# A two-layer graph network: both products with A2 by two levels of Strassen's scheme, streamed from DRAM, with outer sums of A2 made during the attention

## The chip, the core and the metric

The kernel runs on one core of a Trainium2 chip. A core has a matrix engine (TensorE; PE in the profile, its weight loads PEld), a vector engine (VectorE, DVE), an activation engine (ScalarE, ACT), a general engine (GpSimd, POOL) and a queue engine (SyncE, SP). SP and POOL issue the transfers between DRAM and the on-chip memory here, and 16 DMA engines carry them out. Each engine executes its own instructions in their order and waits on semaphores. The metric is the device time of one execution in microseconds; lower is better. All data are float32.

## What is computed

The reference, cut to what matters (N = 3327 rows, D = 512 columns):

```python
h = maximum(layernorm(x), 0)                         # layer 0: attention
q, k, v = h @ Wq.T + bq, h @ Wk.T + bk, h @ Wv.T + bv
x = x + softmax(q @ k.T / sqrt(512) + adj + adj) @ v
X = maximum(layernorm(x), 0)                         # layer 1: graph convolution
A2 = adj + eye(N)
dscale = diagonal(A2) ** -0.5
temp = A2 @ X @ W.T                                  # first product with A2
out = x + relu((dscale[:, None] * A2 * dscale[None, :]) @ temp)   # second
```

`adj` is N by N. The change concerns the two products with `A2`, each N by N times N by 512.

## The kernel before

The rows are cut into 26 tiles of 128 (the last has 127), the columns of `adj` into 7 chunks of 512 (the last has 255). The host also hands in `adjT`, the transpose of `adj`.

*Projection* (`merged`, `h_transposed`, `project`): layernorm, transposes and the products with the weights leave `hT`, `v` and `qh` on chip.

*Attention*, 26 tiles in a loop. `scores(i)` loads a row of `adj` chunks, multiplies (line 211), adds on VectorE (line 213) and takes the exponentials on ScalarE (line 220). The score chunks go through four PSUM buffers `mm`, so TensorE can be four chunks ahead of VectorE. `attend(i)` transposes the weights (line 235), copies each transposed chunk to `pT` on ScalarE or VectorE in turn (line 237), and multiplies with `v` (line 254). Then VectorE finishes the row (line 255), POOL stores it to `x1d` (line 75), and a layernorm follows whose power POOL computes (line 111); ScalarE writes the result into `qh`, where `h1(i)` finds it in layer 1. The loop calls `scores(i + 1)` before `attend(i)`.

*Layer 1*. The first product (line 312) runs over seven column chunks and 26 row tiles; `chunk` loads a 128 by 512 block of `adjT` and adds the identity where the block holds the diagonal (line 285). `temp` multiplies with `W` (line 299) and scales by `sd` = `dscale`. The second product (line 336) loads the same blocks again. At the end of each block ScalarE and VectorE finish four row tiles (lines 344, 345) and POOL stores them.

The kernel is written in the Tile framework: its scheduler fixes the order of each engine's instructions when the program is built, out of the order of the program, its own estimates of durations, and the number of buffers of each tile. A tile with `bufs=1` can't be written again before its last reader is done, a DMA among them.

Of the kernel before, what the change touches and what calls it, by code (L numbers as in the profile page):

```python
# [9 lines left out]
F32 = mybir.dt.float32  # L10
AF = mybir.ActivationFunctionType
ALU = mybir.AluOpType
AX = mybir.AxisListType

P = 128
BW = 512
EPS = 1e-5
LOWEST = -3.4028234e38


@with_exitstack
def graph_layers_kernel(
# [24 lines left out]
    nc = tc.nc  # L47
    N, D = x.shape
    DC = D // P
    NT = (N + P - 1) // P  # L50
    NB = (N + BW - 1) // BW
    TB = BW // P
    scale = 1.0 / math.sqrt(D)

    def rows(i):
        return min(P, N - i * P)

    def width(b):
        return min(BW, N - b * BW)

    def tiles_of(b):
        return range(b * TB, min(NT, (b + 1) * TB))
# [6 lines left out]
    def load(dst, src, n):  # L69
        for a, z in pieces(n):  # L70
            nc.sync.dma_start(dst[a:z], src[a:z])  # L71

    def store(dst, src, n):
        for a, z in pieces(n):
            nc.gpsimd.dma_start(dst[a:z], src[a:z])

    const = ctx.enter_context(tc.tile_pool(name="const", bufs=1))
    held = ctx.enter_context(tc.tile_pool(name="held", bufs=1))
    work = ctx.enter_context(tc.tile_pool(name="work", bufs=2))
    psum = ctx.enter_context(tc.tile_pool(name="psum", bufs=2, space=bass.MemoryType.PSUM))  # L80
    dram = ctx.enter_context(tc.tile_pool(name="dram", bufs=1, space=bass.MemoryType.DRAM))

    ident = const.tile([P, P], F32, name="ident")
    make_identity(nc, ident)
    mhalf = const.tile([P, 1], F32, name="mhalf")
# [7 lines left out]
    qh = [held.tile([P, DC, TB * P if b < NB - 1 else len(tiles_of(b)) * P], F32, name=f"qh{b}")  # L93
          for b in range(NB)]

    def h1(i):
        b, t = divmod(i, TB)
        return qh[b][: rows(i), :, t * P : (t + 1) * P]

    x1d = [dram.tile([rows(i), D], F32, name=f"x1d{i}") for i in range(NT)]  # L100

    def layernorm(dst, src, n):

        st = work.tile([P, 6], F32, name="st")
        nc.vector.bn_stats(st[:n], src)  # L105
        mv = work.tile([P, 2], F32, name="mv")
        nc.vector.bn_aggr(mv[:n], st[:n])
        ve = work.tile([P, 1], F32, name="ve")
        nc.vector.tensor_scalar(ve[:n], mv[:n, 1:2], EPS, None, op0=ALU.add)
        rstd = work.tile([P, 1], F32, name="rstd")  # L110
        nc.gpsimd.tensor_tensor(rstd[:n], ve[:n], mhalf[:n], op=ALU.pow)
        nc.vector.tensor_scalar(dst, src, mv[:n, 0:1], rstd[:n], op0=ALU.subtract, op1=ALU.mult)

    with tc.tile_pool(name="kv", bufs=1) as kv:
        hT = [kv.tile([P, DC, width(b)], F32, name=f"hT{b}") for b in range(NB)]
        v = [kv.tile([P, D], F32, name=f"v{i}") for i in range(NT)]


        with tc.tile_pool(name="proj", bufs=1) as proj:
# [5 lines left out]
            first = [load_x(i) for i in tiles_of(0)]  # L125
            w = {}
# [10 lines left out]
            u = proj.tile([P, DC], F32, name="u")  # L137
# [50 lines left out]
        att = ExitStack()  # L188
# [5 lines left out]
        def scores(i):  # L194
# [12 lines left out]
            for c in range(NB):  # L207
                wd = width(c)
                ps = psum.tile([P, BW], F32, name="mm", bufs=4)
                for d in range(DC):  # L210
                    nc.tensor.matmul(ps[:n, :wd], qh[qb][:, d, t * P : t * P + n], hT[c][:, d, :],  # L211
                                     start=d == 0, stop=d == DC - 1)
                nc.vector.tensor_tensor_reduce(ch[c][:n, :wd], ch[c][:n, :wd], ps[:n, :wd], 2.0, LOWEST,  # L213
                                               op0=ALU.add, op1=ALU.max, accum_out=mx[:n, c : c + 1])
# [28 lines left out]
        def attend(i):  # L243
            n = rows(i)
            _, xt, rs = S[i]
            ps = psum.tile([P, D], F32, name="av")
            sb = transposed(i, 0)
            for c in range(NB):
                now = sb
                if c + 1 < NB:  # L250
                    sb = transposed(i, c + 1)
                for k, j in enumerate(tiles_of(c)):
                    m = rows(j)
                    nc.tensor.matmul(ps[:n], now[:m, k, :n], v[j][:m], start=j == 0, stop=j == NT - 1)  # L254
            nc.vector.scalar_tensor_tensor(xt[:n], ps[:n], rs[:n], xt[:n], op0=ALU.mult, op1=ALU.add)
            store(x1d[i], xt[:n], n)
            y = work.tile([P, D], F32, name="y", bufs=1)
            layernorm(y[:n], xt[:n], n)
            nc.scalar.activation(h1(i), y[:n].rearrange("p (c e) -> p c e", c=DC), AF.Relu)
            del S[i]  # L260

        scores(0)
        for i in range(NT):
            if i + 1 < NT:
                scores(i + 1)
            attend(i)
        att.close()


    with tc.tile_pool(name="conv", bufs=1) as conv:  # L270
        w1 = conv.tile([P, DC, D], F32, name="w1")
        nc.sync.dma_start(w1, w1T.rearrange("(c p) o -> p c o", p=P))
        ts = [conv.tile([P, D], F32, name=f"ts{i}") for i in range(NT)]
        dg = [conv.tile([P, 1], F32, name=f"dg{i}") for i in range(NT)]
        sd = [conv.tile([P, 1], F32, name=f"sd{i}") for i in range(NT)]

        def chunk(j, b, diagonal):

            m, wd = rows(j), width(b)
            a = conv.tile([P, BW], F32, name="a", bufs=12)  # L280
            load(a[:m, :wd], adjT[j * P : j * P + m, b * BW : b * BW + wd], m)
            if j // TB == b:
                t = j % TB
                blk = a[:m, t * P : t * P + m]
                nc.vector.tensor_add(blk, blk, ident[:m, :m])  # L285
                if diagonal:
                    junk = conv.tile([P, P], F32, name="junk", bufs=2)
                    nc.vector.scalar_tensor_tensor(junk[:m, :m], blk, 1.0, ident[:m, :m], op0=ALU.mult,
                                                   op1=ALU.mult, accum_out=dg[j][:m])
                    nc.gpsimd.tensor_tensor(sd[j][:m], dg[j][:m], mhalf[:m], op=ALU.pow)  # L290
            return a

        def temp(b, axt):

            for i in tiles_of(b):
                n, t = rows(i), i % TB
                ps = psum.tile([P, D], F32, name="av")
                for d in range(DC):
                    nc.tensor.matmul(ps[:n], axt[:, d, t * P : t * P + n], w1[:, d, :],  # L299
                                     start=d == 0, stop=d == DC - 1)  # L300
                nc.vector.tensor_scalar(ts[i][:n], ps[:n], sd[i][:n], None, op0=ALU.mult)


        waiting = None
        for b in range(NB):
            wd = width(b)
            acc = [psum.tile([P, BW], F32, name="mm", bufs=4) for _ in range(DC)]
            for j in range(NT):
                m = rows(j)
                a = chunk(j, b, True)  # L310
                for d in range(DC):
                    nc.tensor.matmul(acc[d][:, :wd], h1(j)[:, d, :], a[:m, :wd],  # L312
                                     start=j == 0, stop=j == NT - 1)
                if j == 1 and waiting:
                    temp(*waiting)
            axt = conv.tile([P, DC, BW], F32, name="axt", bufs=2)
            for d in range(DC):
                cp = nc.vector.tensor_copy if d % 2 else nc.scalar.copy
                cp(axt[:, d, :wd], acc[d][:, :wd])  # L319
            waiting = b, axt  # L320


        for b in range(NB):
            its = tiles_of(b)
            acc = [psum.tile([P, D], F32, name="mm", bufs=4) for _ in its]
            res = []
            for i in its:
                xr = conv.tile([P, D], F32, name="x1", bufs=8)
                load(xr, x1d[i], rows(i))
                res.append(xr)  # L330
            for j in range(NT):
                m = rows(j)
                a = chunk(j, b, False)
                for t, i in enumerate(its):
                    n = rows(i)
                    nc.tensor.matmul(acc[t][:n], a[:m, t * P : t * P + n], ts[j][:m],  # L336
                                     start=j == 0, stop=j == NT - 1)
                if j == 1 and waiting:
                    temp(*waiting)
                    waiting = None  # L340
            for t, i in enumerate(its):
                n = rows(i)
                r = conv.tile([P, D], F32, name="r", bufs=4)
                nc.scalar.activation(r[:n], acc[t][:n], AF.Relu, scale=sd[i][:n])  # L344
                nc.vector.tensor_add(r[:n], r[:n], res[t][:n])
                store(out[i * P : i * P + n], r[:n], n)


# [35 lines left out]
```

## Time and profile before

| | |
|---|---|
| Time, median of 3 runs (lowest, highest) | 2730.26 us (2728.12, 2731.69) |
| The profiled execution | 2727.29 us; span of its core 2724.9 us; mean granted TensorE clock 0.997 |
| Projection | up to 213 us of the span |
| Attention, 26 tiles, one each 47.50 us | to 1456 us |
| Idle TensorE at the start of layer 1 | 7.53 us (to 1463.8 us) |
| First product (line 312), busy | 584.4 us |
| Product with `W` (line 299), busy | 90.4 us |
| Second product (line 336), busy | 580.6 us |
| DMA over the span | 172.5 MB, mean 63 GB/s |

"Busy" is the time in which at least one instruction of a group ran; "mean ns of one" is longer for matmuls, since they overlap. A float32 matmul is two MATMUL instructions in the profile (a transpose is one): the 1352 of line 336 are 676 products of a 128 by 128 weight with 512 columns. "Idle before" is the idle time of the engine ahead of a group, with what ended it. The last columns of a row of the windows are the granted TensorE clock (1.00 is full speed), the busy share of the DMA engines and their GB/s.

### The profile page before, as it was taken

To read this page: it belongs to the slowest core of one execution; us is meant where nothing else is said; L and a number is where in the kernel's file an instruction comes from. 1 tells how busy PE (TensorE), PEld (TensorE's weight loads), DVE (VectorE), ACT (ScalarE), POOL (GpSimd) and SP (SyncE) were. 2 spreads that over 40 slices of the span, in tenths; PEclk is the share of its full clock that TensorE was granted. 3 is DMA by queue.
4 is the path that set the end of the run, shared out by engine and by line. 5 is a ranking of instruction groups with operands and counts; after the bars stand their busy time and mean duration, and the time that the engine had idled before them with its cause. 6 is when DMAs were issued, how large, how long until landed. Compare 5 with 4: busy or idle time off the path is not lost.

```text
span 2724.9 us, 17898 instructions
## 1 busy us (share of the span) xinstructions
PE 2697.8 (99%) x7100; PEld 1277.0 (47%) x7100; DVE 387.0 (14%) x983; ACT 237.1 (9%) x591; POOL 74.6 (3%) x138
## 2 busy tenths in 40 slices
PE   8999999999999999999998999999999999999998
PEld 4445444444444445444444444444446544444443
DVE  3322121212122121221211000000000000000000
ACT  1001111121111112111110000000000000000000
POOL 1000000000000000000000000000000000000000
PEclk9999999999999999999999999999999999999999
DMA  3001111111111111111103222222221332333322
GB/s 120 31 8 62 47 41 56 43 52 47 44 51 44 51 41 53 47 47 52 41 25 131 78 62 62 77 60 61 77 56 45 93 106 81 103 108 108 99 65 60
DMA packets 96900, 172.54 MB, mean 63 GB/s; under 512 B 11434, under 2 KB 21415, under 8 KB 96816
## 3 DMA queue, kind: packets, MB, share of 16 engines
q1 hardware_dynamic: 92592, 157.77, 20.4%
q0 software_dynamic: 4224, 13.63, 1.3%
q8 instruction: 55, 0.90, 0.1%
q14 instruction: 29, 0.24, 0.0%
HBM read 157.73 MB, written 13.63 MB: 63 GB/s over the span
## 4 chain that ended last, share of the span: by engine, by line
PE 99%; DMA 1%; DVE 0%; SPq 0%; ACT 0%; issue 0%; POOL 0%; POOLq 0%; ACTq 0%
PE mm L312 21%; PE av L254 21%; PE mm L211 21%; PE mm L336 21%; PE av L299 3%; PE av L176 3%; PE mm L168 3%; PE tp L235 3%; PE mm L143 1%; DMA wk<-in_wk_dram 0%; PE tp L160 0%; DMA a<-in_adjT_dram 0%; PE mm L149 0%; SPq L71 0%; DVE st L105 0%
## 5 line engine op out<-in xcount | busy, mean ns | idle before, releaser
L254 PE MATMUL av<-v,pT 128*128 128x512 f32 (+2 forms) x1352 | 606.2, 593 | 0.6 <-ACT pT L237 0.6
L312 PE MATMUL mm<-a,qh 128*128 128x512 f32 (+3 forms) x1456 | 584.4, 564 | 7.5 <-DVE a L285 7.5
L211 PE MATMUL mm<-hT,qh 128*128 128x512 f32 (+3 forms) x1456 | 588.5, 561 | 0.0
L336 PE MATMUL mm<-ts,a 128*128 128x512 f32 (+2 forms) x1352 | 580.6, 592 | 0.0
L312 PEld LDWEIGHTS mm<-a,qh 128*128 128x128 f32 (+1 forms) x1456 | 277.6, 191 | 314.2 <-issue 308.9
L211 PEld LDWEIGHTS mm<-hT,qh 128*128 128x128 f32 (+1 forms) x1456 | 274.5, 190 | 303.4 <-issue 299.0
L336 PEld LDWEIGHTS mm<-ts,a 128*128 128x128 f32 (+2 forms) x1352 | 256.8, 190 | 323.0 <-issue 323.0
L254 PEld LDWEIGHTS av<-v,pT 128*128 128x128 f32 (+2 forms) x1352 | 246.5, 190 | 261.4 <-issue 254.1
L213 DVE CUSTOM_DVE_ANT_0 s<-s,mm 128x512 f32<-128x512 f32 (+2 forms) x182 | 117.8, 647 | 373.8 <-PE mm L211 370.8
L220 ACT ACTIVATE s<-s,nmx 128x512 f32<-128x512 f32 (+2 forms) x182 | 123.1, 681 | 63.7 <-DVE nmx L216 63.7
L237 ACT COPY pT<-tp 128x512 f32<-128x512 f32 (+1 forms) x104 | 52.1, 501 | 823.7 <-PE tp L235 823.7
L235 PEld LDWEIGHTS tp<-ident,s 128*128 128x128 f32 (+2 forms) x676 | 84.8, 142 | 71.7 <-issue 68.9
L235 PE MATMUL tp<-ident,s 128*128 128x128 f32 (+2 forms) x676 | 99.3, 273 | 0.0
L237 DVE COPY pT<-tp 128x512 f32<-128x512 f32 (+1 forms) x78 | 53.9, 692 | 278.9 <-PE tp L235 278.9
L168 PE MATMUL mm<-hT,M 128*128 128x512 f32 (+1 forms) x224 | 91.5, 562 | 0.0
L299 PE MATMUL av<-w,axt 128*128 128x512 f32 (+1 forms) x208 | 90.4, 592 | 0.0
L176 PE MATMUL av<-wv,hT 128*128 128x512 f32 (+1 forms) x208 | 90.4, 592 | 0.0
L285 DVE TENSOR_TENSOR a<-a,ident 128x128 f32<-128x128 f32 (+1 forms) x52 | 15.2, 292 | 523.7 <-DMA a<-in_adjT_dram 506.7
L344 ACT ACTIVATE r<-mm,sd 128x512 f32<-128x512 f32 (+1 forms) x26 | 17.9, 687 | 570.0 <-PE mm L336 570.0
L319 ACT COPY axt<-mm 128x512 f32<-128x512 f32 (+1 forms) x14 | 7.8, 556 | 661.5 <-PE mm L312 661.5
L299 PEld LDWEIGHTS av<-w,axt 128*128 128x128 f32 (+1 forms) x208 | 39.5, 190 | 49.3 <-issue 49.3
L176 PEld LDWEIGHTS av<-wv,hT 128*128 128x128 f32 (+1 forms) x208 | 39.5, 190 | 49.3 <-issue 49.3
(43 smaller groups left out, 471.2 us busy)
## 6 DMA issues: line engine op xcount, KB each, us to landing
a<-in_adjT_dram SPq DMA_DIRECT2D x300, 256.0 KB, 2.6
s<-in_adj_dram SPq DMA_DIRECT2D x150, 256.0 KB, 2.6
xt<-in_x_dram SPq DMA_DIRECT2D x25, 256.0 KB, 3.0
xr<-in_x_dram SPq DMA_DIRECT2D x25, 256.0 KB, 2.5
x1d<-xr POOLq DMA_DIRECT2D x25, 256.0 KB, 2.3
x<-x1d SPq DMA_DIRECT2D x25, 256.0 KB, 4.2
out_dram<-r POOLq DMA_DIRECT2D x25, 256.0 KB, 4.3
a<-in_adjT_dram SPq DMA_DIRECT2D x50, 127.5 KB, 2.0
```

Source lines behind the costliest of these rows:

```text
L143: nc.tensor.matmul(ps, w["q"][:, c, r * P : (r + 1) * P], w["k"][:, c, :], start=c == 0, stop=c == DC - 1)
L168: nc.tensor.matmul(ps[:, :wd], M[:, c, o * P : (o + 1) * P], hT[b][:, c, :wd], start=c == 0, stop=c == DC - 1)
L176: nc.tensor.matmul(ps[:n], hT[b][:, c, t * P : t * P + n], w["v"][:, c, :], start=c == 0, stop=c == DC - 1)
L211: nc.tensor.matmul(ps[:n, :wd], qh[qb][:, d, t * P : t * P + n], hT[c][:, d, :], start=d == 0, stop=d == DC - 1)
L213: nc.vector.tensor_tensor_reduce(ch[c][:n, :wd], ch[c][:n, :wd], ps[:n, :wd], 2.0, LOWEST, op0=ALU.add, op1=ALU.max, accum_out=mx[:n, c : ...
L220: nc.scalar.activation(ch[c][:n, :wd], ch[c][:n, :wd], AF.Exp, bias=nmx[:n], accum_out=sums[:n, c : c + 1])
L235: nc.tensor.transpose(pt[:m, k, :n], S[i][0][c][:n, k * P : k * P + m], ident[:n, :n])
L237: cp(sb[:, :full, :n], pt[:, :full, :n])
L254: nc.tensor.matmul(ps[:n], now[:m, k, :n], v[j][:m], start=j == 0, stop=j == NT - 1)
L299: nc.tensor.matmul(ps[:n], axt[:, d, t * P : t * P + n], w1[:, d, :], start=d == 0, stop=d == DC - 1)
L312: nc.tensor.matmul(acc[d][:, :wd], h1(j)[:, d, :], a[:m, :wd], start=j == 0, stop=j == NT - 1)
L336: nc.tensor.matmul(acc[t][:n], a[:m, t * P : t * P + n], ts[j][:m], start=j == 0, stop=j == NT - 1)
```

## The change

`adjT` comes in padded with zeros to 3328 by 3328. `A2` is cut twice into 2 by 2, and each level multiplies with seven block products instead of eight, by Winograd's form of Strassen's scheme.

- *Outer sums of A2* (`sums_unit`): four sums of blocks, `S1` to `S4`, made once during the attention, in 104 units of 208 columns: two loads, three additions, one store to `sumd`. Four units follow each `attend` in the program.
- *Outer and inner sums of the right-hand side* (`right_hand`): for each of seven outer products and each pair of row tiles, eight 128-column blocks, stored to `rhs`. Those of the first product follow `attend` of tiles 19 to 24 and the end of the attention; those of the second are made between the steps of layer 1, out of the results of `temp`.
- *Layer 1* (`Step`, `gather`): two products, two halves of the rows, seven outer products, and for each seven steps: six of two row tiles and one of one. A step loads its block of `A2` (or its sum) and of `rhs`, makes the inner sums of `A2` on VectorE, and multiplies 416 columns at a time into seven PSUM banks, one for each inner product (`p8` besides for the last step). `gather` adds the seven banks up into `ct`. `temp` and `finish` use the bank `p8` too; `finish` transposes `ct` back for the output.

The diff, cut to its core:

```diff
+ORDER = ("p5", "p1", "p6", "p7", "p2", "p3", "p4")
+HALF = 13; PAIRS = 6; HW = HALF * P; XW = HW // 2; QW = HW // 4; CW = 208
+    def sums_unit(pool, s, j, c):
+        g = pool.tile([P, 4, CW], F32, name="g")
+        for y in range(2):
...
+            nc.sync.dma_start(g[:, 2 * y : 2 * y + 2, :], src[:, :, c : c + CW])
+            for x in range(2):
+                with_diagonal(g[:, 2 * y + x, :], r0, c0 + x * XW)
+        o = pool.tile([P, 4, CW], F32, name="o")
+        nc.vector.tensor_add(o[:, 0:2, :], g[:, 0:4:3, :], g[:, 1:2, :].to_broadcast([P, 2, CW]))
+        nc.vector.tensor_add(o[:, 2, :], o[:, 1, :], g[:, 0, :])
+        nc.vector.tensor_add(o[:, 3, :], o[:, 2, :], g[:, 2, :])
+        nc.gpsimd.dma_start(sumd[s][j][:, :, c : c + CW], o)
+    def inner(bt):
+        nc.vector.tensor_sub(bt[:, 4], bt[:, 0], bt[:, 1])
...
+    def right_hand(pool, g, products, t, row, written=()):
+        for r in products:
+            what = B_OF[r]
+            if what not in ("T2", "T4"):
+                bt = pool.tile([P, 8, P], F32, name="bt")
+            for k, i in enumerate((HALF - 1,) if t is None else (t, t + PAIRS)):
+                outer(bt[:, 2 * k : 2 * k + 2], what, lambda: row(i), lambda: row(HALF + i))
...
+                inner(bt)
+                nc.gpsimd.dma_start(rhs[g][r][t], bt)
 
+        presum = att.enter_context(tc.tile_pool(name="presum", bufs=1))
             attend(i)
+            for unit in units[i * per_tile : (i + 1) * per_tile]:
+                sums_unit(presum, *unit)
+            if HALF + PAIRS <= i < HALF + 2 * PAIRS:
+                right_hand(presum, 0, ("p5", "p6", "p4", "p1", "p7", "p2", "p3"), i - HALF - PAIRS, h1)
+        right_hand(presum, 0, ("p5", "p6", "p4", "p1", "p7", "p2", "p3"), None, h1)
...
+        with nc.allow_non_contiguous_dma(reason="the diagonal, once"):
+            nc.sync.dma_start(dg, bass.AP(..., ap=[[LD + 1, P], [P * (LD + 1), NT]]))
+            def sums(self):
+                o = self.o = conv.tile([P, 4, QW], F32, name="o", bufs=3)
+                nc.vector.tensor_add(o[:, 0:2, :], a[:, 0:4:3, :], a[:, 1:2, :].to_broadcast([P, 2, QW]))
+                nc.vector.tensor_add(o[:, 2, :], o[:, 1, :], a[:, 0, :])
+                nc.vector.tensor_add(o[:, 3, :], o[:, 2, :], a[:, 2, :])
+            def multiply(self, ps):
...
+                for r, i, m in (
+                    ("p1", 0, a[:, 0, 0]), ("p6", 5, o[:, 2]), ("p7", 6, o[:, 0]), ("p5", 4, o[:, 1]),
+                    ("p2", 2, a[:, 1, 0]), ("p3", 3, o[:, 3]), ("p4", 7, a[:, 1, 1]),
+                ):
+                    nc.tensor.matmul(ps[r][:, :QW], b[:, i], m, ...)
+        def gather(ct, r, ps):
...
+        def finish(ct, i):
+            xr = conv.tile([P, D], F32, name="x1", bufs=2)
+            load(xr, x1d[i], n)
+            pt = banks.tile([P, DC, P], F32, name="p8")
+            for d in range(DC):
+                nc.tensor.transpose(pt[:, d, :], ct[:, d, k * P : (k + 1) * P], ident)
+            o = conv.tile([P, D], F32, name="r", bufs=2)
+            nc.scalar.activation(o[:n], ..., AF.Relu, scale=sd[:n, i : i + 1])
+            nc.vector.tensor_add(o[:n], o[:n], xr[:n])
+            store(out[i * P : i * P + n], o[:n], n)
+        def more(t):
+            temp(cts[0, 1], i)
+            if t is not None:
+                temp(cts[0, 1], i + PAIRS)
+            right_hand(conv, 1, ("p5", *late), t, ts.get, written=("p5",))
+        for k in range(HALF):
+            at(per + k * PAIRS // HALF, lambda k: temp(cts[0, 0], k), k)
+            at(3 * per + k * PAIRS // HALF, lambda k: finish(cts[1, 0], k), k)
+        for k, t in enumerate((*range(PAIRS), None)):
+            at(per + PAIRS + 1 + k, lambda t: right_hand(conv, 1, early, t, ts.get), t)
+            at(2 * per + min(k, PAIRS - 1), more, t)
```

`outer` makes 256 columns with one instruction, of VectorE or (for `B11`, `B21`, `B22`) ScalarE, and `inner` four times 128 columns on VectorE. A step of one row tile multiplies four times 416 columns. `gather` is one copy on ScalarE, eight sums of 416 columns on VectorE and then none, one or three of 1664 columns. In `conv`, `bt` has one buffer, `a` and `b` have six, and `ts` of the second half of the rows has three. The four nested loops of steps call `load` two steps ahead and `sums` one step ahead.

## The prediction

> **What bounds the kernel now.** First the page: busy times, the chain that ended last, the costliest groups.
>
> ```profile
> PE 2697.8 (99%) x7100; PEld 1277.0 (47%) x7100; DVE 387.0 (14%) x983; ACT 237.1 (9%) x591; POOL 74.6 (3%) x138
> ...
> q1 hardware_dynamic: 92592, 157.77, 20.4%
> ...
> PE 99%; DMA 1%; DVE 0%; SPq 0%; ACT 0%; issue 0%; POOL 0%; POOLq 0%; ACTq 0%
> ...
> L312 PE MATMUL mm<-a,qh 128*128 128x512 f32 (+3 forms) x1456 | 584.4, 564 | 7.5 <-DVE a L285 7.5
> ...
> L336 PE MATMUL mm<-ts,a 128*128 128x512 f32 (+2 forms) x1352 | 580.6, 592 | 0.0
> L235 PE MATMUL tp<-ident,s 128*128 128x128 f32 (+2 forms) x676 | 99.3, 273 | 0.0
> ```
>
> TensorE is 99% of the path; the two products of the change take 1165.0 us, with one idle gap of 7.5 us. Nothing else is late: VectorE has 14%. A saved product is saved time, as long as TensorE stays the last.
>
> Second, the groups with their shapes apart, for unit prices; third, the windows; fourth, the DMA view and two lines of the timeline, for what the change leans on and this kernel hardly uses, round trips through DRAM.
>
> ```profile
> L312 PE MATMUL mm<-a,qh 128*128 128x255 f32 x200 | 43.3, 378 | 0.0
> L285 DVE TENSOR_TENSOR a<-a,ident 128x128 f32<-128x128 f32 x50 | 14.6, 292 | 520.7 <-DMA a<-in_adjT_dram 503.7 <-issue 16.7
> L345 DVE TENSOR_TENSOR r<-r,x 128x512 f32<-128x512 f32 x25 | 17.3, 693 | 284.5 <-ACT r L344 284.5
> ```
> ```profile
> 1456.00:1464.00 8.00, 0.47 (x2) 0.23 (x2) 2.88 (x8) 0.63 (x1) 1.68 (x3) 0.70 0.77 259
> 1464.00:1470.00 6.00, 6.00 (x8) 2.47 (x9) 1.81 (x11) 0.00 (x0) 2.55 (x4) 0.54 1.03 390
> ```
> ```profile
> x1d<-xr POOLq DMA_DIRECT2D x25, 256.0 KB, 2.3
> ...
> out_dram<-r POOLq DMA_DIRECT2D x25, 256.0 KB, 4.3
> ...
> x1d<-xr POOLq DMA_DIRECT2D x1, 224.0 KB, 7.0
> ```
> ```profile
> 1003.39 0.75 DVE L255 SCALAR_TENSOR_TENSOR xr<-av,rs,xr 128x512 f32<-128x512 f32 x1 [8.05 <-PE av L254]
> 1004.44 0.58 POOL L75 DMA_DIRECT2D x1d<-xr  x1 [45.95 <-DVE xr L255]
> ```
>
> The windows give 390 GB/s for saturated loads, and a clock of 0.54 behind the 7.5 us gap. A store alone lands in 2.3 us; the same store issued while the loads of layer 1 stream took 7.0. From the end of VectorE's instruction to POOL's issue pass 0.30 us.
>
> **Matmuls.** The built program has 1288 matmuls of 416 columns: 28 outer products of 6 x 7 + 4. A product of 512 columns takes 580.6/676 = 0.859 us, one of 255 takes 43.3/100 = 0.433; a line through them gives 0.700 for 416, so 902 us. `temp` is unchanged (208 MATMULs). The output's 104 transposes at 99.3/676 = 0.147 add 15. TensorE: 902 + 15 - 1165 = **-248**.
>
> VectorE's additions, by L285 and L345, cost 0.158 us + 1.044 ns per column: 0.59 for 416, 0.375 for 208, 0.425 for 256, 1.03 for 832, 1.9 for 1664. Per outer product, 6 x 2.2 of inner sums, 4.8 of `gather` and at most 5.7 of 1664-column sums are 24 us beside 32 us of matmuls: hidden. I allow 0.4 us at each of 28 changes of banks: **+10** (0 to 40).
>
> **Sums of A2 in the attention.** `g` and `o` have one buffer, so unit follows unit: additions 0.59 + 2 x 0.375 and gaps, 1.4 us; then the next addition waits on VectorE's own queue for the later of two round trips. Store: 0.30 + 2.3 for 256 KB + 0.4 for 416 KB at 390 GB/s = 3.0. Loads: two issues and 2.6 = 3.2. A unit is 4.7 us if the two don't disturb each other; each has 416 KB, 1.1 us, and in line it is 5.8; with the 7.0 row it would be 8.7. I take 5.9, near the middle row, because both start together and the loads of `adj` come between. Behind the waiting addition stand the `pT` copies of line 237, the score reductions of line 213 and line 255, so TensorE waits for them after its four buffers. The order of the built program has 13 units before the end of the first tile, ten in each of the next nine, one after. Ten take 59 us, a tile has 47.5 (in the chain in order of time line 211 starts anew at 290.86, 338.36, 385.86): 9 x 11.5, and some 6 in the first tile: **+110** (0 at 4.7 us, +210 at 7).
>
> **Sums of the right-hand side, tiles 19 to 25.** Seven a tile through one `bt`: 0.85 outer and 1.33 inner, then 0.30 + 2.3 + 0.7 for 512 KB; 5.5 us each, 38.5 of 47.5. Hidden but for late copies: **+10** (0; 60 at the middle row).
>
> **Start of layer 1.** All loads of layer 1 wait for the last `right_hand`, since they take the memory of the first layer's pools. From the last product with `v`: row end and layernorm 3.3 us (timeline), one piece with its store 4.6, seven short pieces in series at about 2.6: the last ends at 25. Then `w1` (1 MB), 3328 single elements of the diagonal (no row shows such a load; 0 to 10 us, I take 3, it is small), and 1.4 MB for the first step, 6 us at 390 GB/s, and 6 of latency and first sums: 40 against 7.5 now: **+33** (25 to 45).
>
> **Right-hand sums in layer 1.** They again have one `bt`, and VectorE's queue holds the inner sums of the next steps behind them. (a) Twelve long pieces in outer products 7 and 8; stores beside a stream take 4.3 to 7.0 us, so a piece is 7 to 9 us where a step of 4.9 (11.8 with `temp`) is planned: **+20** (5 to 50). (b) In outer products 14 and 15 the built order puts 26 long pieces ahead of the sums for the third step of product 15, and its `p8` matmul behind the last `temp`. Nine lie beside TensorE's work there. Seventeen remain at 5.5, with 0.9 more for each rebuilt `T1`: 97 us, beside 24 us of `temp`; with the clock and the nine being slower than planned: **+81** (50 to 110). (c) The remaining nine pieces **+12** (0 to 30), and `finish` beside steps **+7** (0 to 15).
>
> **End.** Now 8 us pass from the last matmul to the end. Then `gather` ends at 3, and 13 `finish` go through two `r` buffers: ScalarE 0.69, VectorE 0.69, store 2.6, handovers 0.3, halved: 2.1 us each, 27; then a store and the end, 6: **+29** (20 to 40).
>
> The stream itself: a step loads 0.85 MB of `A2` and 0.52 of `rhs` per 4.9 us, 281 GB/s, 72% of the 390 seen. I price it at nothing; the six buffers cover it.
>
> **The Trainium skill beside this.** "DMA: Bandwidth & Descriptors", "Issuing engines are not separate DMA queues": transfers started by different engines share the 16 engines and interleave; it agrees with the 2.3 and 7.0 rows and speaks against the change. The same page, "Anatomy of one DMA", gives about 2.0 us + bytes/436 GB/s for a store; by that, an estimate, the unit's store is 3.0 us whatever else runs, a unit 4.7, and the attention's term 0. "TensorE: Matmul & The Clock Gate", Part 1, halves the clock after an idle window of about 3.4 us; here 7.5 us idle gave 0.54 in the window behind it. By the rule an idle of 7 us in a tile costs some 3 us more; where VectorE sets the pace, that is hidden.
>
> **Sum.** -248 + 10 + 110 + 10 + 33 + 20 + 81 + 12 + 7 + 29 = +64. The profiled execution took 2727.3 us (2724.9 of span and 2.4 around it), 3.0 less than the median of the three runs: 2727.3 + 64 + 3 = **2794**.
>
> **Rivals.** *Faster: the round trips hide.* With 4.7 us a unit the attention loses nothing, and with 3.3 us for every store the terms of layer 1 are 5, 55, 5 and 0; start 25, end 22, banks 0: -248 + 112 = -136, 2594. For it: the 2.3 row is the median of 25 stores, and the scheduler's order of ten units a tile is what it thinks fits. Against it: the 4.3 and 7.0 rows. The rest unchanged, it decides at a unit of 5.2 us: there the sum is zero. *Slower still: the stream is the bound.* The queue of loads has 20.4% of 16 engines' span for 157.77 MB, 284 GB/s while busy; were that all that a mix of loads and stores reaches, the 901 us would stretch by a tenth or more: +100, 2894. Against it: 390 in the window. *It doesn't do what it says*: 1288 matmuls stand in the built program, so no.
>
> **How the numbers follow.** Forecast 0.60; round trips hide, 0.25 (between 2594 and no change); stream bound 0.12; no change 0.03. So faster by over 0.2% (5.5 us, about what a measurement of this kernel can tell from no change) 0.25, within 0.03, slower 0.72. Range: the attention's term alone spans 210 us, that of (b) 60. Low 2660, which holds the upper half of the hiding case; high 2900, with the stream-bound case.
>
> **What would show it.** Right: matmuls of 902 us; in the first ten tiles a period of 55 to 64 us with TensorE waiting for VectorE (`pT`), whose additions wait for the store of `o`; a hole of 60 to 100 us in the middle of layer 1; 40 us idle at its start; no hole in the steady outer products. Wrong: a period of 47.5 in all tiles, or steps longer than 4.9 us that wait for `a` or `b`.

## The result and the profile after

The changed kernel takes 2838.07 us (median of 4 runs, 2836.17 to 2842.04) beside 2729.70 before (4 runs, 2728.12 to 2731.69): a ratio of 1.0399, 95% interval 1.0381 to 1.0417. It is slower by 108 us, where 64 were predicted (2794 us). The spans of the two profiled executions differ by 2838.1 - 2724.9 = 113.2 us, and the working below is made against these.

First the page of the changed kernel: busy times, the loads' queue, the chain, and the costliest groups.

```profile
PE 2542.8 (90%) x6972; PEld 1271.4 (45%) x6972; DVE 1149.7 (41%) x2471; ACT 271.9 (10%) x683; POOL 190.7 (7%) x315
...
q1 hardware_dynamic: 180540, 360.37, 39.3%
...
issue 15%; POOL 1%; DMA 0%; POOLq 0%; DVE 0%; ACT 0%; ACTq 0%
...
L345 PE MATMUL av<-v,pT 128*128 128x512 f32 (+2 forms) x1352 | 651.2, 629 | 90.3 <-DVE pT L328 89.0
L302 PE MATMUL mm<-hT,qh 128*128 128x512 f32 (+3 forms) x1456 | 596.3, 566 | 37.2 <-DVE mx L304 37.1
L441 PE MATMUL p<-o,b 128*128 128x416 f32 x1344 | 533.4, 517 | 8.1 <-DVE ct L458 5.1
L441 PE MATMUL p<-a,b 128*128 128x416 f32 x1008 | 417.5, 516 | 48.4 <-DVE o L427 39.7
...
L145 DVE TENSOR_TENSOR o<-g 128x416 f32<-128x416 f32 x104 | 61.6, 592 | 316.2 <-DMA sum<-o 270.1
```

TensorE, 99% busy before, now has 90%. The new products (line 441) are cheaper than the old ones, but TensorE now waits for VectorE in the attention (lines 345 and 302), where before it was idle for 0.3 us in all. VectorE in turn stood idle for 270.1 us ahead of the first additions of the units (line 145), until the store of `o` had landed. The chain is of no use here: it runs from the end back along POOL's queue of stores and loses its way ("issue 15%"). What TensorE waited for says it better:

```profile
PE av L345 <- DVE pT L328: 89.0, 22, 8.6
PE p L481 <- DVE ts L483: 63.3, 11, 18.1
PE p L441 <- DVE o L427: 39.7, 1, 39.7
PE mm L302 <- DVE mx L304: 37.1, 18, 4.8
PE p L492 <- ACT r L494: 24.1, 18, 2.9
```

These are the places of the prediction: the units in the attention (first and fourth row), the hole of outer products 14 to 17 (`ts`), the start of layer 1 (one wait of 39.7), the `finish` steps. Outer products are numbered from 0, as in the prediction. The windows put the waits in time; the columns after the engines' busy times are the granted clock, the DMA engines' busy share and GB/s.

```profile
452.10:518.90 66.80, 53.76 (x133) 24.87 (x132) 22.24 (x60) 7.53 (x20) 8.24 (x13) 0.90 0.51 161
955.90:1003.40 47.50, 47.50 (x136) 23.07 (x135) 9.39 (x26) 7.43 (x20) 1.11 (x2) 1.00 0.17 48
...
1647.80:1686.30 38.50, 0.04 (x1) 0.07 (x1) 6.78 (x18) 2.45 (x6) 11.02 (x13) 0.53 0.45 142
...
1753.00:1913.60 160.60, 160.60 (x461) 87.40 (x460) 97.72 (x137) 2.53 (x5) 0.00 (x0) 1.00 0.81 282
...
2255.10:2383.20 128.10, 67.88 (x149) 31.01 (x148) 48.30 (x148) 6.89 (x19) 11.16 (x21) 0.77 0.39 152
...
2796.70:2838.10 41.40, 13.44 (x53) 8.53 (x52) 11.39 (x15) 8.93 (x13) 7.54 (x14) 0.55 0.47 152
```

A tile with units (first row) takes 66.8 us and TensorE works in 53.8 of them; a tile without (second) takes the old 47.5 and TensorE fills it. Five outer products without other work (fourth) take 160.6, TensorE never idle. The third row is the start, the fifth outer product 15, the last the end. Last, one unit in the timeline, and where its transfers land:

```profile
478.40 0.59 DVE L145 TENSOR_TENSOR o<-g 128x416 f32<-128x416 f32 x1 [4.29 <-DMA sum<-o]
...
479.44 0.38 DVE L147 TENSOR_TENSOR o<-o,g 128x208 f32<-128x208 f32 x1
...
479.84 0.88 SPq L140 DMA_DIRECT2D g<-in_adjT_dram  x2
...
480.11 0.71 POOL L148 DMA_DIRECT2D sum<-o  x1 [5.60 <-DVE o L147]
...
484.71 0.59 DVE L145 TENSOR_TENSOR o<-g 128x416 f32<-128x416 f32 x1 [1.40 <-DMA sum<-o]
```
```profile
g<-in_adjT_dram SPq DMA_DIRECT2D x208, 208.0 KB, 3.1
sum<-o POOLq DMA_DIRECT2D x104, 416.0 KB, 4.6
```

From addition to addition 6.31 us pass here. Over the units after the thirteenth the mean is 6.63 (the median 6.38): 1.55 from the first addition's start to the last one's end (a reduction of the scores, line 304, slips in between at times), 0.33 to POOL's issue, 4.60 to the landing, 0.15 to the next addition. Ten of these are the 66.3 us of a tile.

### The profile page after: what moved, and what is told of

It reads as the page before. It is cut to its first block, busy times and chain, and to the rows that moved or that the text cites. A ratio compares the mean times of both kernels' runs of the same rounds, so it can differ in the third digit from the quotient of the medians.

```text
span 2838.1 us, 20558 instructions
## 1 busy us (share of the span) xinstructions
PE 2542.8 (90%) x6972; PEld 1271.4 (45%) x6972; DVE 1149.7 (41%) x2471; ACT 271.9 (10%) x683; POOL 190.7 (7%) x315
## 5 line engine op out<-in xcount | busy, mean ns | idle before, releaser
L345 PE MATMUL av<-v,pT 128*128 128x512 f32 (+2 forms) x1352 | 651.2, 629 | 90.3 <-DVE pT L328 89.0
L441 PE MATMUL p<-o,b 128*128 128x416 f32 x1344 | 533.4, 517 | 8.1 <-DVE ct L458 5.1
L441 PE MATMUL p<-a,b 128*128 128x416 f32 x1008 | 417.5, 516 | 48.4 <-DVE o L427 39.7
L441 PEld LDWEIGHTS p<-o,b 128*128 128x128 f32 x1344 | 256.7, 192 | 227.5 <-issue 201.2
L441 PEld LDWEIGHTS p<-a,b 128*128 128x128 f32 x1008 | 191.8, 191 | 210.9 <-issue 154.1
L425 DVE TENSOR_TENSOR o<-a 128x832 f32<-128x832 f32 x168 | 172.1, 1024 | 251.6 <-PE p L441 181.0
L145 DVE TENSOR_TENSOR o<-g 128x416 f32<-128x416 f32 x104 | 61.6, 592 | 316.2 <-DMA sum<-o 270.1
L481 PE MATMUL p<-w,ct 128*128 128x512 f32 x208 | 104.2, 648 | 63.3 <-DVE ts L483 63.3
L148 POOL DMA_DIRECT2D sum<-o x104 | 74.4, 715 | 667.5 <-DVE o L147 546.6
L426 DVE TENSOR_TENSOR o<-o,a 128x416 f32<-128x416 f32 x168 | 99.3, 591 | 4.8
L427 DVE TENSOR_TENSOR o<-o,a 128x416 f32<-128x416 f32 x168 | 99.2, 591 | 4.7
L328 DVE COPY pT<-tp 128x512 f32<-128x512 f32 (+1 forms) x78 | 53.6, 687 | 112.6 <-PE tp L326 112.6
```

Of the source, the lines that this page charges most:

```text
L328: cp(sb[:, :full, :n], pt[:, :full, :n])
L425: nc.vector.tensor_add(o[:, 0:2, :], a[:, 0:4:3, :], a[:, 1:2, :].to_broadcast([P, 2, QW]))
L426: nc.vector.tensor_add(o[:, 2, :], o[:, 1, :], a[:, 0, :])
L427: nc.vector.tensor_add(o[:, 3, :], o[:, 2, :], a[:, 2, :])
L441: nc.tensor.matmul(ps[r][:, :QW], b[:, i], m, start=self.t == 0, stop=self.t == PAIRS - 1 and r in ("p1", "p5", "p6", "p7"))
L481: nc.tensor.matmul(ps, ct[:, d, k * P : (k + 1) * P], w1[:, d, :], start=d == 0, stop=d == DC - 1)
```

## The experiments

The stage readings below are made alike for each run: the attention ends where VectorE's last row end does, layer 1 runs from its first matmul to its last outer product's, and the end is what follows. The change itself: attention to 1647.8, start 38.4, layer 1 1110.5, end 41.4. The attention's end differs by up to 10 us between runs that have the same code there (1640.3 to 1649.9). Where no number of runs is given, a time is that of one run; the kernel before took 2727.8 to 2730.9 beside them.

### Six units a tile

```diff
-        per_tile = -(-len(units) // NT)
+        per_tile = 6
...
         g = pool.tile([P, 4, CW], F32, name="g")
+        if after is not None:
+            nc.vector.tensor_copy(g[:, 0, 0:1], after[:, 0:1])
```

Only the first unit of a tile gets `after`; it is `y` of `attend(i)`.

> The same 104 units with the same single buffers, but held at six in each of the tiles 1 to 17 (a copy of one column of y into g, ahead of the first unit's loads, ties them to their tile). Theory: the loss in the attention is VectorE's queue, paced by ten round trips of 6.63 us in a tile of 47.5; six are 39.8 and fit, so all tiles take 47.5 to 49, the attention ends 160 to 190 us sooner, 2650 to 2680 in all. Rival (the transfers of the units slow the tile by themselves, wherever they are): the same bytes cost the same 190 us, spread over 17 tiles at some 58 us, 2838. Second rival (the half clock that TensorE gets is on the path): the tiles with units still show it, and the period stays some 5 us above 47.5, 2730.

Measured: 2785.88 us (4 runs; 1.0197 of before, 1.0177 to 1.0218). The attention ends at 1602.5; the 17 tiles with units take 55.4 us at the median (mean 55.6). No expectation holds alone: six units do not fit for nothing, nor do they keep their price. A tile and a part of it, in windows, and three lines of that part:

```profile
630.00:685.50 55.50, 50.50 (x134) 23.89 (x133) 17.42 (x49) 7.54 (x20) 5.43 (x8) 0.94 0.45 142
...
660.30:675.30 15.00, 11.34 (x26) 5.00 (x25) 3.47 (x9) 1.71 (x6) 1.43 (x2) 0.77 0.51 165
```
```profile
666.61 0.59 DVE L147 TENSOR_TENSOR o<-g 128x416 f32<-128x416 f32 x1 [4.68 <-DMA sum<-o]
...
667.94 0.68 DVE L330 COPY pT<-tp 128x512 f32<-128x512 f32 x1
...
668.68 6.78 PE L347 MATMUL av<-v,pT 128*128 128x512 f32 x8 [3.06 <-DVE pT L330]
```

VectorE is busy for 17 of 55 us, so it is not short of time. TensorE is idle for 5.0 us, all of it waiting for copies of `pT` (4.4 for those of VectorE, which stand behind units), and works 3.0 us longer than the 47.5 at a clock of 0.94: the eight matmuls behind the longest wait take 6.78 us, eight at full clock 3.60. So here the slower clock is on the path. In the change itself it seems hidden: ten units alone account for the 66.3. The next question is what exactly stands behind the waiting addition.

### Where a unit's 6.6 us come from

Three runs on the unit itself, with the units as the planner packs them (the planner is Tile's scheduler).

```diff
-        o = pool.tile([P, 4, CW], F32, name="o")
+        o = pool.tile([P, 4, CW], F32, name="o", bufs=2)
...
-        per_tile = -(-len(units) // NT)
+        per_tile = 6
...
+            if i == HALF + PAIRS:
+                first_sums.close()
+                presum = att.enter_context(tc.tile_pool(name="prerhs", bufs=1))
```

The last lines make room for the second `o`; nothing ties the six units to their tile here, and the planner puts 13 before the end of the first tile and nine to eleven into each of the next nine.

> The output tile o of a unit has two buffers, g still one (to make room, the right-hand sums' bt opens after the last unit). Theory (the store's landing is the end that paces a unit): now the loads are, 1.56 of additions, 0.45 to the second issue, 3.78 to its landing and 0.1, so 5.9 a unit in place of 6.63; 104 of them, 75 us off, about 2763. Rival (loads and store are bound by shared bandwidth): the unit stays at 6.6, 2838.

Measured: 2783.92 us. The unit takes 5.99 on average (median 5.87) where the change has 6.63 (6.38), about as expected, and VectorE now waits for the loads:

```profile
DVE o L145 <- DMA g<-in_adjT_dram: 256.0, 81, 5.4
```

The attention ends 53.6 us sooner, not 75: 0.64 us a unit are 67 over 104 units, and where the rest stayed was not worked out. That the store was the last of the two round trips is shown.

```diff
-            nc.sync.dma_start(g[:, 2 * y : 2 * y + 2, :], src[:, :, c : c + CW])
+            if not (s or j or c):
+                nc.sync.dma_start(g[:, 2 * y : 2 * y + 2, :], src[:, :, c : c + CW])
```

> Leaves out the loads of g for all units but the first: the sums of A2 are those of the first unit. Measures the store of o without loads beside it. If the store takes 4.6 us because the unit's two loads run beside it, it falls to 2.7 to 3.1 (the row of 2.3 us for 256 KB and 0.4 more), a unit to 5.0, a tile to 50, some 2670 in all. If the 832-byte pieces of the store set its time, it stays at 4.6, a unit at 6.4 to 6.6, a tile at 65, some 2820.

Measured: 2701.25 us, period 50 to 55, unit 5.26 (median 4.93). The store without the unit's loads:

```profile
sum<-o POOLq DMA_DIRECT2D x104, 416.0 KB, 3.1
```

The median is 3.05 us, against 4.57 with the unit's loads beside it: these neighbours cost 1.5 us. Without them the store in pieces of 832 bytes is 0.35 us over the 2.7 that the prediction worked out for one alone.

```diff
-    sumd = [[dram.tile([P, len(SUMS), XW], F32, name=f"sum{s}_{j}") for j in range(HALF)] for s in range(2)]
+    sumd = [[dram.tile([P, XW // CW, len(SUMS), CW], F32, name=f"sum{s}_{j}") for j in range(HALF)] for s in range(2)]
...
-        nc.gpsimd.dma_start(sumd[s][j][:, :, c : c + CW], o)
+        nc.gpsimd.dma_start(sumd[s][j][:, c // CW], o)
...
```

> The sums lie in DRAM by units, so that the store of o writes 3328 bytes a partition in one piece where it wrote four of 832; the loads of layer 1 that read the sums now read pieces of 832. If the pieces set the store's time, it falls to about 2.8 us, the loads of g decide, 5.9 a unit, some 75 us off the attention; layer 1 may then wait for a, and steps longer than 4.6 us with TensorE waiting for a or o show it. If the loads beside it set the store's time, it stays at 4.6 and nothing changes, 2838.

Measured: 2798.95 us, unit 6.26 (median 6.15), attention to 1608.5, 39 us sooner: between the two.

```profile
g<-in_adjT_dram SPq DMA_DIRECT2D x208, 208.0 KB, 3.7
sum<-o POOLq DMA_DIRECT2D x104, 416.0 KB, 3.7
```

In whole rows the store lands in 3.7 beside loads, where in pieces it took 4.6: beside loads the pieces count. The row of the loads has to be read with care. It is the median over two loads a unit, of which the second takes longer; taken apart, the first has 2.81 us for 2.65 and the second 3.94 for 3.77, so each is only 0.2 slower, and the 3.7 for 3.1 is the median changing from one to the other. VectorE now waits for the loads (269.1 us) and no longer for the store, and the second load's landing paces the unit. Layer 1, which now reads pieces of 832 bytes, keeps its 32.1 us a product.

### Which queue the waiting addition stands in

```diff
-            cp = nc.vector.tensor_copy if c % 2 else nc.scalar.copy
+            cp = nc.scalar.copy
```

> The kernel with six units a tile, and all copies of pT on ScalarE where every second one was on VectorE. With six units a tile the period was 55.4 us, not 47.5. Theory: VectorE has the time (6 x 6.63 and 9), but two copies of pT a tile stand in its queue behind an addition that waits for a store, TensorE waits 5.0 us for them and gets the half clock for some 3 more; with the copies on ScalarE the period is 47.5 to 48.5, the attention ends near 1460 to 1475, some 2650 in all. Rival (units slow the tile by their transfers): the period stays at 55, 2786.

Measured: 2791.84 us, period still 55. The expectation was wrong, and the timeline of one tile says why:

```profile
654.02 0.59 DVE L147 TENSOR_TENSOR o<-g 128x416 f32<-128x416 f32 x1 [4.45 <-DMA sum<-o]
...
655.76 0.72 ACT L313 ACTIVATE s<-s,nmx 128x512 f32<-128x512 f32 x1 [5.10 <-DVE nmx L309]
...
661.10 5.59 PE L347 MATMUL av<-v,pT 128*128 128x512 f32 x8 [5.10 <-ACT pT L330]
```

VectorE waits 4.45 us for a store; the last reduction `nmx` stands behind it; ScalarE's exponentials wait for `nmx`; the copy stands behind the exponentials; TensorE waits 5.10 for the copy. The wait changed its engine and kept its length. The loss did not go with the copies, so the next run moves the waiting additions themselves.

```diff
-        nc.vector.tensor_add(o[:, 0:2, :], g[:, 0:4:3, :], g[:, 1:2, :].to_broadcast([P, 2, CW]))
-        nc.vector.tensor_add(o[:, 2, :], o[:, 1, :], g[:, 0, :])
-        nc.vector.tensor_add(o[:, 3, :], o[:, 2, :], g[:, 2, :])
+        nc.gpsimd.tensor_add(o[:, 0:2, :], g[:, 0:4:3, :], g[:, 1:2, :].to_broadcast([P, 2, CW]))
+        nc.gpsimd.tensor_add(o[:, 2, :], o[:, 1, :], g[:, 0, :])
+        nc.gpsimd.tensor_add(o[:, 3, :], o[:, 2, :], g[:, 2, :])
```

The tie's copy and the addition of the diagonal go to GpSimd too.

> The kernel with six units a tile, with the additions of a unit (and the copy that ties it) on GpSimd in place of VectorE; copies of pT as they were. With the copies on ScalarE the period had stayed at 55: ScalarE's exponentials wait for VectorE's last reduction, which stands behind a waiting addition, and the copies behind the exponentials. Theory: what costs is an addition that waits at the head of a queue through which all of the attention's work goes; on GpSimd's queue only the reciprocal root of a layernorm and the stores stand behind it, so the period is 47.5 to 49, whatever the additions take there (no row has one of this size; a unit may take 6 to 8 us, six of them 36 to 48), the attention ends near 1460 to 1490, 2650 to 2680 in all. Rival (the units' transfers beside TensorE's and VectorE's work): 55, 2786.

Measured: 2656.67 us, the attention to 1471.0. The tile that took 55.5 on VectorE:

```profile
630.00:677.50 47.50, 47.50 (x136) 23.07 (x135) 9.22 (x25) 7.43 (x20) 20.31 (x31) 1.00 0.47 150
```

The same transfers (150 GB/s), longer additions (1.06 and twice 0.62 us, for 0.59 and 0.37), a unit of 7.42, and no loss in 13 of 17 tiles; four took up to 4 more, for which no reason is shown. The rival, that the transfers slow the tile, has fallen. The run does take two things off VectorE's queue, the waits and the additions' own 8 us a tile (busy 9.2 for 17.4). Of the two the waits weigh more: in the lines of the first run above, the copy of `pT` was held up for 6.0 us, 4.7 of wait and 1.3 of additions. No run has one without the other. The fourth corner, GpSimd without the tie:

> The other corner: the additions of the units on GpSimd as in the run before, but not tied to their tiles, so that the planner puts eleven or twelve into each of the first nine tiles. Theory (units in line, each 7.4 us on GpSimd, 1.06 + 2 x 0.62 of additions, then the store and the loads): eleven are 81 us; the root of a tile's layernorm stands behind them on GpSimd, y waits for it on VectorE, and VectorE's next reductions behind y, so a tile takes 80 to 85, the attention ends 250 to 330 us later than 1457, 2890 to 2970 in all. Rival (off VectorE the units cost nothing, however many stand together): 47.5, 2650.

Measured: 2976.81 us, tiles of 82 to 88, the attention to 1786.9.

```profile
ACT qh L352 <- DVE y L203: 480.9, 9, 55.7
DVE y L203 <- POOL rstd L202: 399.0, 10, 47.2
PEld mm L302 <- DVE mx L304: 311.0, 9, 38.6
```

VectorE waits up to 47 us for the layernorm's `rstd`, which stands behind eleven units on POOL, and TensorE for VectorE. Eleven units of 7.43 are 82 us, the length of the tile. So neither the engine nor the number alone decides: ten a tile on VectorE 66, eleven on GpSimd 83, six on VectorE 55, six on GpSimd 47.5 to 51.6. What costs is what stands behind a waiting instruction, and for how long.

### The hole in outer products 14 to 17

```diff
-                bt = pool.tile([P, 8, P], F32, name="bt")
+                bt = pool.tile([P, 8, P], F32, name="bt", bufs=2 if pool.name == "conv" else 1)
```

> The changed kernel, with two buffers for the right-hand sums' bt in layer 1 and nothing else. Theory (the hole of 85 us in outer products 14 to 17 is the round trip of one bt, 2.1 us of VectorE and 2.9 of store for each of 35 pieces, 26.8 us for the five of a step): T4 is made in the place of T2 and still waits for its store, the other pieces overlap; a step's five take some 15 us, the hole shrinks by 50 to 60, 2780 in all. Rival (VectorE's own work, or the order in which the pieces stand ahead of the sums for TensorE): the pieces take the same time, the hole stays near 85, 2838.

Measured: 2769.04 us; outer products 14 to 17 are 23.3 us over 4 x 32.1 and the 44.7 of `temp` (13 x 4 products of 512 columns at 0.859), where the change has 85.6, and TensorE's wait for `ts` falls from 63.3 to:

```profile
PE p L481 <- DVE ts L483: 15.9, 6, 4.7
```

One buffer's round trip was 62 of the 86 us of the hole. Products 7 to 9 gain 7.4 us by the same edit.

Spreading the pieces over products 15 to 17 as well, for which all of `ts` is kept:

```diff
-            right_hand(conv, 1, ("p5", *late), t, ts.get, written=("p5",))
+            right_hand(conv, 1, ("p5", "p6", "p4"), t, ts.get, written=("p5",))
...
+            for later, r in enumerate(("p7", "p2", "p3")):
+                at(2 * per + (later + 1) * (PAIRS + 1) + k, lambda t, r: right_hand(conv, 1, (r,), t, ts.get), t, r)
```

> As the kernel with two bt, and the pieces of p7, p2 and p3 made one outer product after another (products 15, 16 and 17) in place of all in product 14; the second half of ts is kept for that. Theory (too many pieces in one place, each with its round trip): 14 pieces stay beside the 13 temp, the rest is 7 a product at 2.1 us of VectorE, which has 12 us free in each of 32; the hole falls to 5 to 25 us, 2760 to 2780 in all. Rival (the pieces cost the same wherever they are): no better than with two bt alone.

Measured: 2776.75 us, 29.5 us of the hole left, none gained over the two buffers: the rival's result, but not by its reason. Product 14 takes 76.6, as TensorE alone would, and product 16 now 52.0 where 32.1 are work: ten long pieces stand together there, six of `p2` and four of `p3`.

```profile
2355.63 0.71 ACT L165 COPY bt<-ts 128x256 f32<-128x256 f32 x2 [8.55 <-DMA b1p<-bt]
...
2358.20 0.50 ACT L454 COPY s<-p 128x416 f32<-128x416 f32 x1
...
2358.75 1.76 PE L441 MATMUL p<-a,b 128*128 128x416 f32 x2 [10.09 <-ACT s L454]
```

The copy with which `gather` empties the first bank stands on ScalarE behind copies of `p3` that wait for a `bt`, and TensorE waits 10.1 us for it. What the same pieces would cost if they were held apart was not tried.

### The end

```diff
-            xr = conv.tile([P, D], F32, name="x1", bufs=2)
+            xr = conv.tile([P, D], F32, name="x1", bufs=4)
...
-            o = conv.tile([P, D], F32, name="r", bufs=2)
+            o = conv.tile([P, D], F32, name="r", bufs=4)
```

> The changed kernel, with four buffers each for x1 and r of the last step. Theory (the end, 41 us from the last product's matmul, is 13 finish through two r, 2.2 us each): with four the engines' own 0.7 us and 0.55 of issue are the pace, about 1 us each, the end 23 to 28, 2822 in all. Rival (the landing of the stores, one after another on GpSimd's queue): 41, 2838.

Measured: 2813.82 us. The end is 32.5, between the two; product 21, beside which the other `finish` lie, takes 37.8 in place of 49.8; the attention ended 7.5 us sooner, which is its own spread. Of the end's pitch of 2.2 us, 1.89 are left:

```profile
2802.28 0.69 ACT L494 ACTIVATE r<-p,sd 127x512 f32<-127x512 f32 x1 [1.21 <-PE p L492]
```

ScalarE now waits for the transposes, which wait for the one bank `p8` that ScalarE reads.

### All together

Units on GpSimd, five or six in each of tiles 0 to 18; three `bt` and four `x1` and `r` in layer 1; the loads of `w1` and the diagonal moved behind the first steps, six `finish` beside the last outer product (their columns are final by then), and:

```diff
-        right_hand(presum, 0, ("p5", "p6", "p4", "p1", "p7", "p2", "p3"), None, h1)
         att.close()
+        with tc.tile_pool(name="short", bufs=4) as short:
+            right_hand(short, 0, ("p5", "p6", "p4", "p1", "p7", "p2", "p3"), None, h1)
...
+            if k == 8:
+                w1 = conv.tile([P, DC, D], F32, name="w1")
...
+        for k in range(PAIRS):
+            at(4 * per - PAIRS - 1 + k, lambda k: finish(cts[1, 1], HALF + k), k)
...
-        for k in range(HALF):
-            finish(cts[1, 1], HALF + k)
+        for k in range(PAIRS, HALF):
+            finish(cts[1, 1], HALF + k, f"p{1 + k % 7}")
```

> Units on GpSimd, five or six in each of tiles 0 to 18; three bt in layer 1; the last tile's short right-hand pieces through four buffers once the scores' memory is free; w1 and the diagonal loaded behind the first steps; four x1 and r, the last seven finish over seven banks, and six finish beside the last outer product, since their columns are final by then. By the measured terms: attention 1457 to 1465; start 22 to 30 in place of 38.4; layer 1: 28 x 32.1 and 26 temp 89, and 26 finish's transposes 13, with 15 to 30 of the hole left and 5 to 10 in products 7 to 9, 1015 to 1040; end 18 to 25. Sum 2512 to 2560, against 2727 before. Rival (the streams' loads and stores, now closer together, or the faster end, bring a new wait): over 2600.

Measured: 2529.95 us (4 runs, 2528.76 to 2531.62), 0.9274 of before (0.9259 to 0.9290): faster than both. Attention to 1459.7, start 20.2, layer 1 1029.5, end 20.4. The page and TensorE's waits:

```profile
PE 2461.7 (97%) x6972; PEld 1248.1 (49%) x6972; DVE 1015.5 (40%) x2119; ACT 271.6 (11%) x683; POOL 450.7 (18%) x686
```
```profile
PE p L435 <- DMA b<-b0p: 21.4, 1, 21.4
PE p L475 <- DVE ts L477: 19.7, 6, 5.6
```

TensorE is at 97% again, and its longest waits are the start and what is left of the hole.

## Why the prediction was right, and where its size was off

The steps, in us of the profiled executions, and what the stages measured:

| Step | Predicted | Measured |
|---|---|---|
| Matmuls and output transposes | -248 | 28 x 32.12 = 899 for 902; -251 with the 15 |
| Bank changes | +10 | 0 (TensorE never idle in products 2 to 6) |
| Sums of A2 in the attention | +110 | +189 (1647.8 - 1457.1, less the next row) |
| Right-hand sums, tiles 19 to 25 | +10 | +2 |
| Start of layer 1 | +33 | +32 (wait of 39.7, less 7.5); the diagonal's load, taken as 3, has 7.5 in it |
| (a) products 7 to 9 | +20 | +15.5 |
| (b) and (c) products 14 to 17, and `finish` beside steps | +100 | +85.6 + 10.1 |
| End, without its transposes | +29 | 41.4 - 8 - 7.6 = +26 |

The measured column adds up to 109 of the 113; most of the rest is the first outer product, 34.6 for 32.1.

*Right:* the matmuls; that the two levels save what they should and that VectorE's sums in layer 1 hide; that the round trips of single buffers bring more back; and each of the places. Of "What would show it" nearly all came in as told: the first ten tiles wait for `pT` behind additions that wait for the store of `o`, a hole of 85.6 us in the middle of layer 1, 40 us idle at its start, steady products without holes. Only the period, 64.9 to 67.5 us, lies above the 55 to 64 given. The rival "round trips hide" fell with the period of 66; "the stream is the bound" fell with 160.6 us of five products at 282 GB/s without an idle moment; the change did what it says.

*Off:* one term, the sums of A2 in the attention, 79 of the error; the other terms together were too high by some 30, most of it in the bank changes, the right-hand sums of the attention and (a), so that by luck the sum is nearer than its largest term. The mechanism was right and the unit mis-sized: 5.9 was taken, 6.63 measured. After 1.4 of additions and 0.3 to the issue, the 5.9 leave 4.2 for a store that shares with the loads; measured were 1.55, 0.33, 4.60, and 0.15 to the next addition. Each part was short by a little, and the number of units multiplies it. The nine tiles with ten units lost 169.4 and not 103.5: of these 66 us, 90 x 0.73 = 66 are the unit's size. The first tile, where 13 units lie before its end, lost 26.8 and not 6: 13 x 0.73 = 9 of it is the unit's size, the rest the 6, for which the prediction gave no sum. The tile after these ten won 6.9 back, which it did not foresee. A small slip besides: at the start of layer 1, 3.3 + 4.6 + 7 x 2.6 are 26 and not 25.

The rule weighed in the prediction, from the Trainium skill's "DMA: Bandwidth & Descriptors" ("Anatomy of one DMA"), is right for the store without the unit's loads: by it, an estimate, 3.0 us; the run without loads has 3.05. With loads beside it 4.57 were measured, as the same page's "Issuing engines are not separate DMA queues" would have it, since different engines' transfers share the 16 engines; that section gives no figure. The slower clock behind idle time ("TensorE: Matmul & The Clock Gate", Part 1) was weighed as hidden: in the change it seems so (66.3 us are ten units), with six units a tile it is not (3.0 us of the tile's 55.5).

What the prediction did not see is the other half of its own term: it took the loss for the sum of the units' time over the tile. With six units, whose sum is 6 x 6.63 = 40 us of 47.5, the tile still lost 8, mostly by what stood behind the waits.

The Trainium skill's "GPSIMD Engine Reference", "4.1 Engine selection", sends elementwise additions to VectorE, GpSimd being about twice as slow with two inputs. The trace has 1.06 us for 0.59, and yet the kernel with six units there is 129 us shorter than the one with six on VectorE: the table ranks the engines by speed, and here it counted more which queue had to wait.

## What to carry to other kernels

Before a round trip is put on an engine that the critical path goes through, list what stands behind its wait, on that engine and on those that wait for it; a wait at the head of such a queue costs even where the engine is mostly idle. Price a store and a load that start together as sharing, and multiply small errors by the number of trips. Where a planner orders the work, hold the background work to so much a tile, give it an engine with little behind it, and give each round trip a second buffer; by this the same arithmetic went from 4% slower to 7% faster.

## What the runs showed of the hardware

- A 416 KB store in 832-byte pieces lands in 3.05 us without the unit's two loads of 208 KB and in 4.57 beside them; in 3328-byte pieces beside the loads in 3.67, with either load 0.2 us slower (medians).
- The 3328 single elements of the diagonal (13 KB) take 6.6 to 7.5 us to land, and 10.9 in the last run, where their load lies behind the first steps; the prediction took 3.
- An addition of 416 columns takes 1.06 us on GpSimd and 0.59 on VectorE; of 208 columns 0.62 and 0.37. In a tile with six units on GpSimd, TensorE, VectorE and ScalarE were busy for 47.50, 9.22 and 7.43 us, in one without units for 47.50, 9.39 and 7.43.
